# Attention value products: one piece instead of two for some key tiles

## The chip, the cores and the metric

The kernel runs on 1 core of one Trainium2 chip. The metric is the device time of one execution in microseconds (us). The engines are named as in the profile: PE (TensorE, matrix products), PEld (its weight loads), DVE (VectorE), ACT (ScalarE), POOL (GpSimd) and SP (SyncE, which issues transfers).

## The reference, cut to what matters

Four layers work on one sequence of 2048 rows of 256 numbers, each added to its input: attention (16 heads, 4 key and value heads, rotary positions, biases), a gated MLP with dequantised 4-bit weights, attention with 16 key and value heads, and the same MLP again. The change is in the attention, which for each head is

```python
scores = jnp.einsum('bhqd,bhkd->bhqk', q, k) / jnp.sqrt(hd)
scores = jnp.where(causal[None, None], scores, -inf)
attn = jax.nn.softmax(scores, axis=-1)
out = jnp.einsum('bhqk,bhkd->bhqd', attn, v)
```

Nothing in the arithmetic of the reference changes here; only how the last line is cut into instructions does.

## The kernel before, in words

**Units.** Queries are taken in four blocks `b` of 512 rows (`TB`), heads in four groups `g` of four. A pair (b, g) is a unit; each attention layer runs its 16 units in order. Keys come in tiles of 128 rows: unit (b, g) has 4(b + 1) of them, of which the last four are diagonal. A diagonal tile masks the causal triangle and has 512, 384, 256 and 128 queries left (`q0` = 0, 128, 256, 384). I call these four k0 to k3. All other tiles are full: 512 queries.

**Two sweeps.** A softmax needs the largest score of each row. `max_steps` (line 776) computes scores with queries on the partitions (L787), masks diagonal pieces (L762), and DVE takes maxima (L799). A maximum is as wide as its keys: 512 for keys of earlier blocks, 128 to 512 on the diagonal. `gather` (L811 to L822) makes the row maxima, and `turn` transposes them on PE (L835), from where ACT copies them to `mT` (L841). `value_steps` (line 848) then computes the scores again with keys on the partitions. `pair(kt, p)` handles key tile `kt` and heads 2p and 2p + 1 of the group: PE puts the negated maxima into PSUM (L884) and adds the scores (L889) and, on the diagonal, the masks (L762); ACT takes the exponential into a tile `e` (L901). One pair is two heads of 512 queries. The maxima of a unit are made beside the value sweep of the unit before it.

**Value products.** `values(half)` (line 853) multiplies the exponentials of key tile `kt - 1` with its values (L869), after `pair(kt, half)`. Four products, one for each head, write four groups of 32 rows of one accumulator `ps_av`. In the profile each of these four is two matmuls, so one call is 8 records. Before the change a tile with 384 or 512 queries is cut: `values(0)` does queries up to 256, `values(1)` the rest. A tile with 256 or 128 queries is done whole in `values(0)`. The last unit of a layer, (3, 3), which has no maxima of a next unit beside it, does all its tiles whole in `values(1)`.

**Buffers.** Score tiles of both sweeps, `ps_s`, share three buffers in PSUM, used in turn: a fourth tile waits until the exponential (ACT) or the maximum (DVE) of an earlier one has been read. `e` has four buffers, two key tiles' worth.

**Order.** It is written by hand. `run` (line 974) makes for each unit a list of main steps, two for a key tile (p = 0, 1), and a list of side steps: maxima of the next unit, preparation of the next block, the output projection. `weave` runs the scores of a main step, then its share of side steps, then `values`. No side steps fall on the last three main steps of a unit (`rest=3`): k2's second pair and both of k3. The masks of a diagonal tile are put off (`owed`) and issued at the next `settle`, which every `pair` and `values` call and some maxima begin with. The last tile's products and the copy of `ps_av` (`end`) come after the first pair of the next unit; in the last unit they follow directly, and the MLP (L1086) comes next on PE.

Of the kernel before, what the change touches and what calls it, by code (L numbers as in the profile page):

```python
# [27 lines left out]
NG = NH // 4  # L28
MLP = 2048
NFC = MLP // P  # L30
TB = 512
NB = S // TB
# [48 lines left out]
def tile_hybrid_layers(  # L81
# [40 lines left out]
    def ps_s():  # L122
        return psum.tile([P, 2, 512], F32, tag="s", name="ps_s", bufs=3)

    def ps_av():
        return psum.tile([P, 512], F32, tag="av", name="ps_av")

    def ps_m():
        return psum.tile([P, 512], F32, tag="m", name="ps_m")
# [22 lines left out]
    once = first_w.enter_context(tc.tile_pool(name="once", bufs=1))  # L152
# [258 lines left out]
    class Attention:  # L411
# [11 lines left out]
        def __init__(self, first, wqkv):  # L423
            self.first, self.wqkv = first, wqkv
            self.kvh = NKV if first else NH
            self.npair = NKV if first else NH // 2
            self.krows = self.kvh * HD
            self.kT, self.vv, self.qT, self.mT, self.att = {}, {}, {}, {}, {}
            self.q_d, self.k_d = {}, {}
            self.owed, self.after = [], []  # L430

        def place(self, pool, b):

            kvh = self.kvh
            self.kT[b] = pool.tile([P, self.npair, TB], F32R, tag=f"kT{b}", name=f"kT{b}")
            v_b = pool.tile([P, NT, kvh * VW + V_PAD], F32, tag=f"v{b}", name=f"v{b}")
            nc.gpsimd.memset(v_b[:, :, kvh * VW :], 0.0)
            ones = v_b[:, :, : kvh * VW].rearrange("p t (h c) -> p t h c", c=VW)
            nc.gpsimd.memset(ones[:, :, :, HD : HD + 1], 1.0)
            self.vv[b] = v_b  # L440
# [335 lines left out]
        def max_steps(self, b, g):  # L776

            held = {}

            def scores(i, c, p):  # L780
                if not held:
                    held["mx"] = self.wk.tile([P, NT, 4, NB], F32, tag="mx", name="mx")
                w = TB if c < b else (i + 1) * P
                self.settle("max")
                pt = ps_s()
                for r in range(2):
                    nc.tensor.matmul(  # L787
                        pt[:, r, :w],
                        lhsT=self.qT[b, g][64 * r : 64 * r + 64, p, i * P : (i + 1) * P],
                        rhs=self.key_rows(c, g, p, r, slice(0, w)),  # L790
                        start=True, stop=(c < b),
                    )

                def masked():
                    self.add_mask(pt, 0, w - P)
                    reduced()

                def reduced():
                    nc.vector.tensor_reduce(  # L799
                        held["mx"][:, i, 2 * p : 2 * p + 2, c], pt[:, :, :w], AX.X, ALU.max  # L800
                    )

                if c == b:
                    self.owed.append(("max", masked))
                else:
                    reduced()

            def gather():
                self.settle()
                nm = self.wk.tile([P, NT, 4], F32, tag="nm", name="nm")  # L810
                nc.vector.tensor_reduce(  # L811
                    nm, held["mx"][:, :, :, : b + 1], AX.X, ALU.max, negate=True
                )

                to = m_pad[:, :, :, :6].rearrange("q t r (p s) -> q t p r s", s=3)
                rest = nm.rearrange("q t (p r) -> q t p r", r=2)

                nc.vector.tensor_tensor(to[:, :, :, :, 0], rest, rest, ALU.max)
                less = self.wk.tile([P, NT, 2, 2], F32, tag="rest", name="rest")
                nc.vector.tensor_tensor(less, rest, to[:, :, :, :, 0], ALU.subtract)  # L820
                nc.vector.tensor_tensor(to[:, :, :, :, 1], less, less, ALU.max)
                nc.vector.tensor_tensor(  # L822
                    to[:, :, :, :, 2], less, to[:, :, :, :, 1], ALU.subtract
                )

            def turn():
                pt = ps_m()


                for _ in range(4 if (b, g) <= (1, 0) else 0):  # L830
                    nc.tensor.matmul(
                        pt, lhsT=sel[:, 0, :], rhs=nothing, start=True, stop=True
                    )
                for i in range(NT):
                    nc.tensor.matmul(  # L835
                        pt[:, i * P : (i + 1) * P],
                        lhsT=m_pad[:, i].rearrange("p r c -> p (r c)"), rhs=ident_b,
                        start=True, stop=True,
                    )
                self.mT[b, g] = self.wk.tile([P, TB], BF16, tag="mT", name="mT")  # L840
                nc.scalar.copy(self.mT[b, g], pt)  # L841


            tiles = [(i, c) for c in range(b + 1) for i in range(NT)]
            steps = [lambda i=i, c=c, p=p: scores(i, c, p) for i, c in tiles for p in range(2)]
            return steps + [gather], turn

        def value_steps(self, b, g):

            nk = NT * (b + 1)  # L850
            held = {"pending": []}

            def values(half):


                self.settle()
                kt, q0, es_ = held["pending"][0]
                whole = (b, g) == (NB - 1, NG - 1)
                few = whole or TB - q0 <= TB // 2
                if half == 1:  # L860
                    held["pending"].pop(0)
                if few and half != whole:
                    return
                if kt == 0 and half == whole:
                    held["av"] = ps_av()
                own = slice(q0, TB) if few else slice(*((q0, TB // 2), (TB // 2, TB))[half])
                for j in range(4):
                    h = g if self.first else 4 * g + j
                    nc.tensor.matmul(  # L869
                        held["av"][32 * j : 32 * j + 32, own],  # L870
                        lhsT=self.vv[kt // NT][:, kt % NT, h * VW : h * VW + 32],
                        rhs=es_[j // 2][:, j % 2, own],
                        start=(kt == 0 and half == whole), stop=(kt == nk - 1),
                    )

            def pair(kt, p):
                q0 = max(0, kt - NT * b) * P
                diagonal = kt >= NT * b
                keys = slice((kt % NT) * P, (kt % NT + 1) * P)
                self.settle()  # L880
                pt = ps_s()

                for r in range(2):
                    nc.tensor.matmul(  # L884
                        pt[:, r, q0:], lhsT=sel[64 * r : 64 * r + 64, p, :],
                        rhs=self.mT[b, g][64 * r : 64 * r + 64, q0:], start=True, stop=False,
                    )
                for r in range(2):
                    nc.tensor.matmul(  # L889
                        pt[:, r, q0:], lhsT=self.key_rows(kt // NT, g, p, r, keys),  # L890
                        rhs=self.qT[b, g][64 * r : 64 * r + 64, p, q0:],
                        start=False, stop=not diagonal,
                    )
                e = self.wk.tile([P, 2, TB], F32, tag="e", name="e", bufs=4)

                def masked():
                    self.add_mask(pt, 1, q0)
                    exponentials()

                def exponentials():  # L900
                    nc.scalar.activation(e[:, :, q0:], pt[:, :, q0:], AF.Exp, scale=QK_SCALE)  # L901

                if diagonal:
                    self.owed.append(("exp", masked))
                else:
                    exponentials()
                if p == 0:
                    held["es"] = [e]
                else:
                    held["pending"].append((kt, q0, held["es"] + [e]))  # L910

            def end():
                values(0)
                values(1)
                o = pre.tile([P, TB], F32, tag="o", name="o")
                nc.scalar.copy(o, held["av"])
                held["o"] = o
# [19 lines left out]
            for kt in range(nk):  # L937
                for p in range(2):
                    scored = lambda kt=kt, p=p: pair(kt, p)
                    steps.append((scored, lambda p=p: values(p)) if kt else scored)  # L940
# [296 lines left out]
```

## Time and profile before

| what | value |
|---|---|
| median of 3 runs | 1833.45 us |
| lowest and highest | 1830.45 and 1834.42 us |
| span of the profiled execution | 1830.9 us |
| time of the profiled execution beside its span | not listed apart from the span |
| PE busy | 1748.1 us, 95% |
| DVE busy | 1123.5 us, 61% |
| ACT busy | 808.1 us, 44% |
| value products (L869) | 4384 records, 350.7 us busy |
| maxima (L799) | 640, 660.3 us busy |
| exponentials (L901) | 640, 568.8 us busy |

Attention lies at about 40 to 560 us and 950 to 1490 us of the span, the MLPs after each. Busy times count an engine as busy from the start of an instruction to its modelled end. A timeline row gives the start of a group of equal instructions, how long the group lasted, engine, line, operation and tiles, the number of records, and in brackets idle time of the engine before it with what ended it. Since matmuls overlap, the cost of a group to PE is read from its start to the start of the next group.

### The profile page before, as it was taken

Reading aid. Unit: us, or ns where it says so; the run is one execution under the profiler, and the core shown is the slowest. Engines: PE = TensorE matmul, PEld = TensorE weight load, DVE = VectorE, ACT = ScalarE, POOL = GpSimd, SP = SyncE. Lnnn points to the kernel's source line nnn. Section 1 sums busy time; section 2 is a strip of 40 time slices with the busy share of each in tenths; the row PEclk is TensorE's granted clock in tenths of the full one; section 3 lists DMA queues with packets and bytes.
Section 4 is the critical chain, followed back from the end, with each engine's and each line's share of the span. In section 5 each row is a group of like instructions: output and inputs, shape, how many; then the busy total and the mean of one; then the engine's idle time right before and its main releaser. Section 6 shows DMA issues by size and latency. Waiting matters only on the chain.

```text
span 1830.9 us, 31568 instructions
## 1 busy us (share of the span) xinstructions
PE 1748.1 (95%) x13313; PEld 913.3 (50%) x13313; DVE 1123.5 (61%) x1679; ACT 808.1 (44%) x1080; POOL 239.8 (13%) x444
## 2 busy tenths in 40 slices
PE   8888899899999999999998999999999999999999
PEld 4444444444443474746464444444444445655646
DVE  5576887887884626262644767767877626354442
ACT  2435556566667313131314455655666753132221
POOL 4122202110013101012101000000000001111010
PEclk9899999999999999999999999999999999999999
DMA  5240400120002100005006132032000000000000
GB/s 139 68 93 32 94 24 30 48 50 24 19 13 76 52 1 0 1 0 125 2 1 117 24 76 53 22 60 59 13 13 2 11 37 1 12 3 9 7 6 12
DMA packets 43134, 65.40 MB, mean 36 GB/s; under 512 B 14000, under 2 KB 21040, under 8 KB 42736
## 3 DMA queue, kind: packets, MB, share of 16 engines
q1 hardware_dynamic: 34352, 47.37, 9.0%
q0 software_dynamic: 7680, 15.48, 4.9%
q8 instruction: 105, 1.72, 0.4%
q10 hardware_dynamic: 960, 0.52, 0.1%
q14 instruction: 37, 0.30, 0.1%
HBM read 43.45 MB, written 17.83 MB: 33 GB/s over the span
## 4 chain that ended last, share of the span: by engine, by line
PE 74%; DVE 15%; ACT 7%; issue 2%; DMA 1%; POOL 0%; ACTq 0%; DVEq 0%; SPq 0%; POOLq 0%
PE ps_s L1086 24%; DVE mx L799 12%; PE ps_av L869 10%; PE ps_s L884 7%; PE ps_s L787 6%; PE ps_m L1111 6%; PE ps_av L1111 6%; ACT e L901 5%; PE ps_s L889 5%; PE ps_m L504 2%; PE ps_m L963 2%; PE ps_s L762 1%; ACT mT L841 1%; PE ps_s L504 1%; PE ps_m L923 1%
## 5 line engine op out<-in xcount | busy, mean ns | idle before, releaser
L799 DVE TENSOR_REDUCE mx<-ps_s 128x2 f32<-128x1024 f32 (+3 forms) x640 | 660.3, 1061 | 216.7 <-PE ps_s L762 109.0
L901 ACT ACTIVATE e<-ps_s 128x1024 f32<-128x1024 f32 (+3 forms) x640 | 568.8, 898 | 374.1 <-PE ps_s L889 219.5
L869 PE MATMUL ps_av<-e,v 128*32 128x256 f32 (+2 forms) x4384 | 350.7, 391 | 0.0
L889 PE MATMUL ps_s<-qT,kT 64*128 64x512 f32 (+3 forms) x1280 | 333.8, 519 | 0.0
L787 PE MATMUL ps_s<-kT,qT 64*128 64x512 f32 (+3 forms) x1280 | 266.5, 418 | 34.2 <-DVE mx L799 15.3
L884 PE MATMUL ps_s<-mT,sel 64*128 64x512 bf16 (+3 forms) x1280 | 229.9, 353 | 26.1 <-ACT mT L841 11.0
L1086 PE MATMUL ps_s<-xnT,wg 128*128 128x512 f32 x512 | 240.9, 593 | 0.0
L1086 PE MATMUL ps_s<-xnT,wu 128*128 128x512 f32 x512 | 240.6, 592 | 0.0
L884 PEld LDWEIGHTS <-sel 64*128 64x128 bf16 x1280 | 75.5, 93 | 252.4 <-issue 241.8
L787 PEld LDWEIGHTS ps_s<-kT,qT 64*128 64x128 f32 x1280 | 127.6, 185 | 142.8 <-ACT e L901 67.3
L1092 ACT ACTIVATE t<-ps_s 128x512 f32<-128x512 f32 x128 | 76.3, 596 | 243.9 <-PE ps_s L1086 243.7
L1095 ACT ACTIVATE t<-t 128x512 f32<-128x512 f32 x128 | 80.6, 629 | 199.0 <-DVE t L1094 199.0
L1094 DVE TENSOR_TENSOR t<-ps_s,t 128x512 f32<-128x512 f32 x128 | 88.2, 689 | 123.3 <-POOL t L1093 121.1
L1086 PEld LDWEIGHTS ps_s<-xnT,wu 128*128 128x128 f32 x512 | 97.3, 190 | 122.5 <-issue 122.5
L1093 POOL TENSOR_SCALAR t<-t 128x512 f32<-128x512 f32 x128 | 79.0, 618 | 534.4 <-ACT t L1092 530.8
L1086 PEld LDWEIGHTS ps_s<-xnT,wg 128*128 128x128 f32 x512 | 95.1, 190 | 104.2 <-issue 102.5
L1096 DVE SCALAR_TENSOR_TENSOR t<-t,ps_s 128x512 f32<-128x512 f32 x128 | 88.0, 687 | 89.0 <-ACT t L1095 89.0
L869 PEld LDWEIGHTS ps_av<-e,v 128*32 128x32 f32 x4384 | 87.3, 108 | 93.2 <-issue 78.9
L889 PEld LDWEIGHTS ps_s<-qT,kT 64*128 64x128 f32 x1280 | 128.4, 195 | 0.0
L1111 PE MATMUL ps_m<-wd,inter 128*128 128x256 f32 x512 | 114.5, 380 | 0.0
L1111 PE MATMUL ps_av<-wd,inter 128*128 128x256 f32 x512 | 114.5, 380 | 0.0
L1111 PEld LDWEIGHTS ps_av<-wd,inter 128*128 128x128 f32 x512 | 96.7, 190 | 17.1 <-issue 4.5
(147 smaller groups left out, 1192.8 us busy)
## 6 DMA issues: line engine op xcount, KB each, us to landing
qT<-h SPq DMA_DIRECT2D x248, 64.0 KB, 2.2
kT<-h POOLq DMA_DIRECT2D x88, 128.0 KB, 5.8
h<-high SPq DMA_DIRECT2D x24, 256.0 KB, 2.1
h<-low SPq DMA_DIRECT2D x24, 256.0 KB, 3.1
wd<-wd_kept SPq DMA_DIRECT2D x2, 2048.0 KB, 8.2
wd_kept<-dq_d SPq DMA_DIRECT2D x4, 512.0 KB, 2.7
out<-x SPq DMA_DIRECT2D x16, 128.0 KB, 1.7
x<-x SPq DMA_DIRECT2D x3, 512.0 KB, 7.5
```

Source lines behind the costliest of these rows:

```text
L787: nc.tensor.matmul(pt[:, r, :w], lhsT=self.qT[b, g][64 * r : 64 * r + 64, p, i * P : (i + 1) * P], rhs=self.key_rows(c, g, p, r, slice(0, w)),
L799: nc.vector.tensor_reduce(held["mx"][:, i, 2 * p : 2 * p + 2, c], pt[:, :, :w], AX.X, ALU.max)
L869: nc.tensor.matmul(held["av"][32 * j : 32 * j + 32, own], lhsT=self.vv[kt // NT][:, kt % NT, h * VW : h * VW + 32], rhs=es_[j // 2][:, j % ...
L884: nc.tensor.matmul(pt[:, r, q0:], lhsT=sel[64 * r : 64 * r + 64, p, :], rhs=self.mT[b, g][64 * r : 64 * r + 64, q0:], start=True, stop=False,)
L889: nc.tensor.matmul(pt[:, r, q0:], lhsT=self.key_rows(kt // NT, g, p, r, keys), rhs=self.qT[b, g][64 * r : 64 * r + 64, p, q0:], start=Fals ...
L901: nc.scalar.activation(e[:, :, q0:], pt[:, :, q0:], AF.Exp, scale=QK_SCALE)
L1086: nc.tensor.matmul(pt[:, k, :], lhsT=w[:, c, fc * P : (fc + 1) * P], rhs=self.xnT[b][:, c, :], start=(c == 0), stop=(c == 1),)
L1093: nc.gpsimd.tensor_scalar(t, t, GELU_A, 1.0, ALU.mult, ALU.add)
L1094: nc.vector.tensor_tensor(t, gate, t, ALU.mult)
L1095: nc.scalar.activation(t, t, AF.Tanh, scale=GELU_C)
L1096: nc.vector.scalar_tensor_tensor(t, t, 1.0, gate, ALU.add, ALU.mult)
L1111: nc.tensor.matmul(po[:, :D], lhsT=inter[:, fc, i * P : (i + 1) * P], rhs=wd[:, fc, :], start=(fc == 0), stop=(fc == NFC - 1),)
```

## The change

A flag `wide` is set while a step issues a maximum over more than 256 keys and cleared by each `pair`. At `values(0)` it is decided how the tile is done: with fewer than 512 queries, whole in `values(0)`; with 512 queries and no wide maximum since the pair before it, whole in `values(1)`; else in two halves as before. The special case of the last unit is gone.

```diff
             def values(half):
                 self.settle()
                 kt, q0, es_ = held["pending"][0]
-                whole = (b, g) == (NB - 1, NG - 1)
-                few = whole or TB - q0 <= TB // 2
+                if half == 0:
+                    held["late"] = q0 == 0 and not self.wide
+                    held["once"] = q0 > 0 or held["late"]
                 if half == 1:
                     held["pending"].pop(0)
-                if few and half != whole:
+                if held["once"] and half != held["late"]:
                     return
-                if kt == 0 and half == whole:
+                opening = kt == 0 and half == held["late"]
+                if opening:
                     held["av"] = ps_av()
-                own = slice(q0, TB) if few else slice(*((q0, TB // 2), (TB // 2, TB))[half])
+                own = slice(q0, TB)
+                if not held["once"]:
+                    own = slice(*((0, TB // 2), (TB // 2, TB))[half])
```

In the order of the built program this joins 62 tiles: k1 (384 queries) of every unit but the last of each layer, 30 in all, now whole in `values(0)`; and 32 tiles of 512 queries outside the last units, now whole in `values(1)`. In the two last units the full tiles and k0 stay as they were, while k1 and k2, already whole, move from `values(1)` to `values(0)`, that is, one pair earlier; k3 comes in `end` as before. All other engines have the same instructions in the same order, and each score tile reuses the buffer of the same predecessor, except at one place.

More of the change, by code (lines that the diff above doesn't have):

```diff
@@ L430, in __init__ @@
             self.owed, self.after = [], []
+            self.wide = False
         def place(self, pool, b):
@@ L785, in scores @@
                 pt = ps_s()
+                self.wide = self.wide or w > TB // 2
                 for r in range(2):
@@ L872, in values @@
                         rhs=es_[j // 2][:, j % 2, own],
-                        start=(kt == 0 and half == whole), stop=(kt == nk - 1),
+                        start=opening, stop=(kt == nk - 1),
                     )
@@ L880, in pair @@
                 self.settle()
+                self.wide = False
                 pt = ps_s()
```

## Prediction

> **What bounds the kernel now.** I began with the page's busy line and its chain of work that ended last.
>
> ```profile
> PE 1748.1 (95%) x13313; PEld 913.3 (50%) x13313; DVE 1123.5 (61%) x1679; ACT 808.1 (44%) x1080; POOL 239.8 (13%) x444
> ...
> PE 74%; DVE 15%; ACT 7%; issue 2%; DMA 1%; POOL 0%; ACTq 0%; DVEq 0%; SPq 0%; POOLq 0%
> ```
>
> PE is the bound, but not alone: in the attention the chain hops over DVE maxima (12% of the span on L799) and ACT exponentials (5% on L901). The question at each joined tile is therefore whether PE was short of time there, or was filling a wait with half a tile.
>
> The price of a group comes from the PE timeline, start to next start. The last unit has whole tiles already:
>
> ```profile
> 1459.99 1.07 PE L869 MATMUL ps_av<-e,v 128*32 128x512 f32 x8
> 1460.99 0.39 PE L884 MATMUL ps_s<-mT,sel 64*128 64x512 bf16 x2
> 1461.03 0.58 PE L889 MATMUL ps_s<-qT,kT 64*128 64x512 f32 x2
> 1461.45 0.39 PE L884 MATMUL ps_s<-mT,sel 64*128 64x512 bf16 x2
> 1461.49 0.58 PE L889 MATMUL ps_s<-qT,kT 64*128 64x512 f32 x2
> 1462.00 1.07 PE L869 MATMUL ps_av<-e,v 128*32 128x512 f32 x8
> ```
>
> 512 queries cost 1.00 us (1459.99 to 1460.99). The same way, 384 cost 0.79 (1485.77 to 1486.56), 256 cost 0.57 and 128 cost 0.35. Going from scores to products costs 0.09 more than going on to the next scores: 1461.49 to 1462.00 against 1461.03 to 1461.45; after masks it is 0.16 against 0.07.
>
> **The change part by part.** *On PE alone.* A joined full tile saves 2 x 0.57 - 1.00 = 0.14, a joined k1 saves 0.35 + 0.57 - 0.79 = 0.13, and each saves one passage of 0.09: about 0.23 us. 62 tiles give 14.3 us, if PE never waits.
>
> A page speaks for more: the Trainium skill, "TensorE: Matmul & The Clock Gate", Back-to-back issue gap, gives a sustained 81 ns a matmul at 128 columns and 131 ns at 512. Interpolated to 98 ns at 256, an estimate, 16 x 98 - 8 x 131 ns is 0.52 us a tile and 32 us for 62. The rows above have 71 and 125 ns a record and decide.
>
> *The tail of a unit (30 k1 tiles).* This is (0,3,2), layer, block and group counted from 0, from k2's first pair:
>
> ```profile
> 553.47 0.28 PE L884 MATMUL ps_s<-mT,sel 64*128 64x256 bf16 x2
> ...
> 553.88 0.43 PE L869 MATMUL ps_av<-e,v 128*32 128x128 f32 x8
> 554.23 0.28 PE L884 MATMUL ps_s<-mT,sel 64*128 64x256 bf16 x2
> ...
> 554.64 0.64 PE L869 MATMUL ps_av<-e,v 128*32 128x256 f32 x8
> 555.21 0.23 PE L884 MATMUL ps_s<-mT,sel 64*128 64x128 bf16 x2
> ...
> 555.56 0.64 PE L869 MATMUL ps_av<-e,v 128*32 128x256 f32 x8
> 556.13 0.40 PE L835 MATMUL ps_m<-ident_b,m_pad 128*128 128x128 bf16 x4
> ```
>
> ```profile
> 554.81 0.60 ACT L901 ACTIVATE e<-ps_s 128x512 f32<-128x512 f32 x1 [0.17 <-PE ps_s L762]
> ```
>
> k2's products at 555.56 need the exponential of k2's second pair. It begins 0.33 after that pair's masks (554.48 to 554.81), lasts 0.60, and the half of k1 at 554.64 covers it. After the change: 384 queries at 553.88, k2's second pair at 554.67, its masks at 554.92, its exponential 555.25 to 555.85. Nothing is left between but k3's first pair: at 554.99, masks at 555.18, k2's products at 555.34. Two of their four heads need the second exponential; PE gets there at 555.62, waits until 555.90 (0.05 after the end, as PE follows ACT at 556.57 + 0.59 to 557.20), and is through at 556.19, against 556.13. So the 0.23 becomes a wait, and 0.06 is lost. Side steps can't cover it, there are none here. Of the 30 tails, 12 show PE waiting afterwards for m_pad from DVE (0.14 to 0.94 us); there it costs nothing. The other 18 cost 18 x 0.06 = 1.1 us.
>
> *The two last units.* k2's products lose the cover of k3's second pair, k3's that of k2's. Walked from 1485.07 with the same steps: k1's products 1485.47, k2's second pair 1486.26, its exponential 1486.82 to 1487.42, second half of k2's products at 1487.47, k3's second pair 1487.76, its exponential 1488.27 to 1488.65, last products until 1488.88. Before, the MLP's first matmul starts at 1488.13. That is 0.75 a layer, 1.5 us; the MLP is PE's, so nothing hides it.
>
> *The 32 full tiles.* With the first half gone, the second pair comes 0.57 + 0.09 = 0.66 earlier, if its score buffer is free. This is (1,3,1), where two narrow maxima stand behind the first pair:
>
> ```profile
> 1394.65 0.39 PE L884 MATMUL ps_s<-mT,sel 64*128 64x512 bf16 x2
> ...
> 1395.60 0.64 PE L869 MATMUL ps_av<-e,v 128*32 128x256 f32 x8
> 1396.44 0.39 PE L884 MATMUL ps_s<-mT,sel 64*128 64x512 bf16 x2 [0.20 <-ACT e L901]
> ...
> 1397.19 0.64 PE L869 MATMUL ps_av<-e,v 128*32 128x256 f32 x8
> ```
>
> ```profile
> 1395.37 1.02 ACT L901 ACTIVATE e<-ps_s 128x1024 f32<-128x1024 f32 x1 [0.49 <-PE ps_s L889]
> ```
>
> First pair and two maxima hold all three buffers; the second pair waits for the first's exponential, 1396.39, with or without a half tile at 1395.60. That half was free. Afterwards the whole tile stands at 1397.19 and costs 1.00 instead of 0.57: 0.43 lost. Five tiles are so: the late ones of (1,3,0), (1,3,1), (1,3,2), (0,2,2), (1,2,2): 2.15 us. Three more ((0,2,3), (1,2,3), (1,1,0)) lose it too, but 0.16 of it meets a wait that stands behind (404.12 + 0.46 to 404.73): 3 x 0.27 = 0.81.
>
> Where one maximum or none follows the first pair, the second pair does come 0.66 earlier, and the next maximum then waits for the first's exponential. (0,3,1), tile at 497.80: the second pair starts at 497.70 instead of 498.37, the maximum at 498.72 (exponential 497.65 to 498.67) instead of 498.83; the products move from 499.39 to 499.28 and end at 500.28; before, the next pair started at 500.17. 0.11 lost. Walked alike: (0,3,2) 0.13, (0,3,0) 0.26, (0,1,3) and (1,1,3) 0.21 each, (0,2,0) and (1,2,0), two tiles each, 0.10 for both, (1,2,1), two tiles, 0.27, (1,1,1)'s first 0.34. Together 1.73 for 12 tiles.
>
> Two tiles have long side work of PE in a step ((0,2,1) and (1,1,1)'s second) and keep the gain: -0.46. In the two at 479.58 and 526.75, DVE then has maxima queued up, PE's 0.31 is hidden: 0. (0,1,0), (0,1,1) and the six k0 tiles of block 0 stand among long preparation; each lies between -0.23 (free gain) and +0.43 (class above), I take 0, since 10 of their 16 halves lie off the chain. Full tiles: 2.15 + 0.81 + 1.73 - 0.46 = 4.2 us.
>
> Again the skill, "Perfetto Trace Analysis", Matmuls: groups should rotate through PSUM banks so that evacuation overlaps the next matmuls, and larger matmuls are more efficient. The first half is what the split did at 1395.60, the second what the change does; by the rows the first is worth 0.57 there, the second 0.14.
>
> *Sum.* 1.1 + 1.5 + 4.2 = 6.8 us on the span of 1830.9, 1837.7. The page has no other time of that execution; the median is 2.55 above its span and I keep that distance: **1840.2 us**, +0.37%. DMAs, DVE, ACT and POOL keep their instructions and order; maxima that come 0.1 to 0.5 earlier wait for nothing else.
>
> **Rivals.** *Faster: PE is the bound and takes the saving.* For it: 95% busy; 45 of the 62 tiles have a half on the chain. 45 x 0.23 = 10.4, so 1823. It decides if the exponentials that I make late are found done; against it, they need to be 0.28 (tails) to 0.6 us (full tiles) earlier, and ACT, with 44% busy, is not late by its own queue but follows PE's masks by a steady 0.33. *Same: tails gain, full tiles lose.* If the wait at 555.62 isn't there, 18 tails give -0.23 each, -4.1, against 4.2 of the full tiles, with the last units about 0: 1833.5. Point: 0.28 us of ACT. *Slower still: the clock.* TensorE's granted clock is 0.51 between 44 and 58 us and 1.00 before; the joined tiles take PE work out of just such thin stretches of block 0. One more such stretch of 14 us costs up to 7 us: 1847; one less, as much in gain. *That it doesn't do what it says* is out: the built order has the 62.
>
> **How the numbers follow.** Forecast 0.58, faster 0.12, same 0.22, clock 0.08. A measurement tells 0.2% or 3.7 us from no change: 1829.8 to 1837.1 is "same". Slower is 0.58 + 0.08 = 0.66, same 0.22, faster 0.12. The forecast's own range: tails 0 to 30 x 0.06 = 1.8, the eight open tiles -1.8 to +3.4, the rest within 2 us: 1836 to 1846. The range takes in the same case and leaves the faster one out: 1830 to 1846.
>
> **What will show it.** Records of the value products (L869, L875 after) fall by 62 x 8 = 496 to 3888. In the tail, products of 256 should split with about 0.3 us between their second and third head; at (1,3,1) the gap before the second pair should be some 0.85 us, ended by ACT; the MLP should start 0.75 later behind each last unit. I am wrong if PE's idle time by "ACT e" does not grow by some 10 us, or if the clock has other stretches below 0.6.

## The result and the profile after

The changed kernel takes 1848.07 us (median of 4 runs, 1847.57 to 1848.66). Four runs of the kernel before have a median of 1832.32 us (1830.45 to 1834.42). The ratio is 1.0088, with a 95% interval of 1.0073 to 1.0102: slower by 15.75 us, where 6.8 had been forecast.

The profiled span grew by 14.9 us, from 1830.9 to 1845.8. The page of the kernel after:

```profile
PE 1751.4 (95%) x12801; PEld 904.3 (49%) x12817; DVE 1124.6 (61%) x1679; ACT 804.9 (44%) x1080; POOL 239.8 (13%) x444
...
PE 76%; DVE 13%; ACT 8%; issue 2%; DMA 1%; POOL 0%; ACTq 0%; SPq 0%; DVEq 0%; POOLq 0%
...
L875 PE MATMUL ps_av<-e,v 128*32 128x256 f32 (+3 forms) x3888 | 355.4, 419 | 0.8 <-ACT e L908 0.8
```

PE does 496 products fewer (its line has 512 records fewer, but its weight loads fell by 496: 16 records are missing from the trace) and is busy 3.3 us *longer*; its idle time (span less busy) grew by 11.6 us, from 82.8 to 94.4. Together that is the 14.9. So there are two questions: who makes PE wait, and why do fewer products take longer? The waits of PE answer the first. The columns are waiting operation, what ended the wait, total us, times, longest. The kernel before:

```profile
PE ps_s L787 <- DVE mx L799: 15.3, 34, 1.3
PE ps_s L787 <- ACT e L901: 15.0, 36, 1.3
...
PE ps_s L884 <- DVE mx L799: 4.7, 14, 0.5
PE ps_m L835 <- DVE m_pad L822: 4.5, 10, 0.9
PE ps_s L884 <- ACT e L901: 4.2, 15, 0.6
```

The kernel after, the same view:

```profile
PE ps_s L789 <- ACT e L908: 19.1, 46, 1.3
PE ps_s L789 <- DVE mx L801: 16.8, 36, 1.3
...
PE ps_s L891 <- ACT e L908: 8.1, 16, 1.2
PE ps_s L891 <- DVE mx L801: 7.4, 20, 0.8
...
PE ps_m L837 <- DVE m_pad L824: 1.5, 4, 0.6
...
PE ps_av L875 <- ACT e L908: 0.8, 4, 0.2
```

Waits for exponentials grew by 8.8 us (19.2 to 28.0), those for maxima by 4.2, and those for `m_pad` fell by 3.0. Nearly all wait at *score* matmuls (L789, L891), which wait for a score buffer. Products themselves wait for only 0.8.

Where in the span is it? I took the times of each unit's `turn` and of each MLP's first matmul in both traces, and the growth of their difference:

| stretch | predicted | measured |
|---|---|---|
| layer 0, start and block 0 | 0 | +4.55 |
| layer 0, blocks 1 to 3 | 5.3 for both layers | +3.72 |
| layer 0, last unit | 0.75 | +1.23 |
| layer 1, block 0 | 0 | +0.34 |
| layer 1, blocks 1 to 3 | (above) | +3.89 |
| layer 1, last unit | 0.75 | +1.21 |
| sum | 6.8 | +14.94 |

Every stretch lost at least what was predicted. The extra comes from block 0 of layer 0 (4.55), from blocks 1 to 3 (2.3) and from the last units (0.9).

**The tail.** This is (0,3,2) on the PE timeline of the kernel after, from k2's first pair to `turn`, and its exponentials on ACT:

```profile
561.43 0.28 PE L891 MATMUL ps_s<-mT,sel 64*128 64x256 bf16 x2
...
561.83 0.85 PE L875 MATMUL ps_av<-e,v 128*32 128x384 f32 x8
562.62 0.28 PE L891 MATMUL ps_s<-mT,sel 64*128 64x256 bf16 x2
...
562.93 0.22 PE L891 MATMUL ps_s<-mT,sel 64*128 64x128 bf16 x2
...
563.27 1.20 PE L875 MATMUL ps_av<-e,v 128*32 128x256 f32 x8
564.41 0.40 PE L837 MATMUL ps_m<-ident_b,m_pad 128*128 128x128 bf16 x4
```

```profile
563.20 0.87 ACT L908 ACTIVATE e<-ps_s 128x512 f32<-128x512 f32 x2 [0.60 <-PE ps_s L763]
```

k2's products stand for 1.20 us, where the same 8 records took 0.64 before, and no wait is named. The single records tell why. Before, the four heads' first passes start at 555.561, 555.568, 555.575 and 555.581: side by side, 7 ns apart. After, two start at 563.273 and 563.280, their second passes at 563.513 and 563.520, and only at 563.847 and 563.854 come the other two heads, whose exponential had not been read. Each pair of heads takes the 0.57 us that all four took. The tail is 2.98 us long instead of 2.66.

**The last unit** of layer 1 loses in the same way, at k2 and again at k3, on the PE timeline after:

```profile
1500.64 1.20 PE L875 MATMUL ps_av<-e,v 128*32 128x256 f32 x8
...
1502.12 0.41 PE L875 MATMUL ps_av<-e,v 128*32 128x128 f32 x4
1502.73 0.41 PE L875 MATMUL ps_av<-e,v 128*32 128x128 f32 x4 [0.19 <-ACT e L908]
1503.07 1.13 PE L1093 MATMUL ps_s<-xnT,wg 128*128 128x512 f32 x2
```

**A full tile** of (1,3,1), the one that the prediction showed:

```profile
1407.13 0.39 PE L891 MATMUL ps_s<-mT,sel 64*128 64x512 bf16 x2
...
1408.92 0.39 PE L891 MATMUL ps_s<-mT,sel 64*128 64x512 bf16 x2 [0.77 <-ACT e L908]
...
1409.67 1.07 PE L875 MATMUL ps_av<-e,v 128*32 128x512 f32 x8
```

The half tile that had stood in the gap is gone, the gap stays until the exponential ends, and the whole tile comes behind it: 1.79 from the first to the second pair, as before (1394.65 to 1396.44), and 1.00 of products afterwards instead of 0.57.

### The profile page after: what moved, and what is told of

The parts are those of the page before. It is cut to its first block, busy times and chain, and to the rows that moved or that the text cites. A ratio compares the mean times of both kernels' runs of the same rounds, so it can differ in the third digit from the quotient of the medians.

```text
span 1845.8 us, 30560 instructions
## 1 busy us (share of the span) xinstructions
PE 1751.4 (95%) x12801; PEld 904.3 (49%) x12817; DVE 1124.6 (61%) x1679; ACT 804.9 (44%) x1080; POOL 239.8 (13%) x444
## 4 chain that ended last, share of the span: by engine, by line
PE 76%; DVE 13%; ACT 8%; issue 2%; DMA 1%; POOL 0%; ACTq 0%; SPq 0%; DVEq 0%; POOLq 0%
PE ps_s L1093 23%; PE ps_av L875 12%; DVE mx L801 10%; PE ps_s L891 7%; PE ps_s L789 6%; PE ps_m L1118 6%; PE ps_av L1118 6%; ACT e L908 5%; PE ps_s L896 5%; PE ps_m L505 2%; PE ps_s L763 2%; PE ps_m L970 2%; ACT mT L843 1%; PE ps_s L505 1%; PE ps_m L930 1%
## 5 line engine op out<-in xcount | busy, mean ns | idle before, releaser
L875 PE MATMUL ps_av<-e,v 128*32 128x256 f32 (+3 forms) x3888 | 355.4, 419 | 0.8 <-ACT e L908 0.8
L789 PE MATMUL ps_s<-kT,qT 64*128 64x512 f32 (+3 forms) x1280 | 266.3, 417 | 39.5 <-ACT e L908 19.1
L891 PE MATMUL ps_s<-mT,sel 64*128 64x512 bf16 (+3 forms) x1280 | 229.8, 353 | 32.0 <-ACT mT L843 11.0
L891 PEld LDWEIGHTS <-sel 64*128 64x128 bf16 x1280 | 75.8, 93 | 263.5 <-issue 254.2
L789 PEld LDWEIGHTS ps_s<-kT,qT 64*128 64x128 f32 x1280 | 127.7, 185 | 148.0 <-ACT e L908 70.4
L875 PEld LDWEIGHTS ps_av<-e,v 128*32 128x32 f32 x3888 | 81.2, 108 | 102.6 <-issue 78.0
L1118 PEld LDWEIGHTS ps_av<-wd,inter 128*128 128x128 f32 x512 | 96.7, 190 | 17.1 <-issue 4.5
```

What stands on the lines that cost most here:

```text
L789: nc.tensor.matmul(pt[:, r, :w], lhsT=self.qT[b, g][64 * r : 64 * r + 64, p, i * P : (i + 1) * P], rhs=self.key_rows(c, g, p, r, slice(0, w)),
L875: nc.tensor.matmul(held["av"][32 * j : 32 * j + 32, own], lhsT=self.vv[kt // NT][:, kt % NT, h * VW : h * VW + 32], rhs=es_[j // 2][:, j % ...
L891: nc.tensor.matmul(pt[:, r, q0:], lhsT=sel[64 * r : 64 * r + 64, p, :], rhs=self.mT[b, g][64 * r : 64 * r + 64, q0:], start=True, stop=False,)
L1118: nc.tensor.matmul(po[:, :D], lhsT=inter[:, fc, i * P : (i + 1) * P], rhs=wd[:, fc, :], start=(fc == 0), stop=(fc == NFC - 1),)
```

## The experiments

The variants change the decision at `values(0)`; variants 5, 10 and 11 change something else as well or instead. The rule of the kernel before, written in the terms of the changed code, is

```python
last = (b, g) == (NB - 1, NG - 1)
held["late"] = last
held["once"] = held["late"] or TB - q0 <= TB // 2
```

and the edits below say what differs from it. The kernel before was run along; its medians over the three groups of runs were 1833.04, 1833.23 and 1832.95 us. Theory A: two heads cost PE what four cost, so a late exponential in a tail costs a second group. Theory B: a pair of heads costs half a group, as I had predicted. C: the surplus is the clock ("half clock" below is a granted clock of 0.5). D, formed after the first four runs: a transfer in block 0 of layer 0 is delayed.

**1. Only k1, blocks 1 to 3.**

```diff
-held["once"] = held["late"] or TB - q0 <= TB // 2
+held["once"] = last or TB - q0 <= TB // 2 or (b > 0 and q0 > 0)
```

> Only k1 of the units in blocks 1 to 3 (24 tiles, the last units left out) is joined, in values(0). Theory A, that the wait for the exponential cuts k2's products into two groups of two heads, each as long as a group of four (0.57 us): 15 tails bound by PE lose 0.32 each, 4.8 us, and the tails that wait for m_pad nearly nothing: +4.5 to +5.5. Theory B, the prediction's, that two heads cost half of four: 15 x 0.06, +0.5 to +1.5. Rival that joining itself pays: -3 or less.

Measured: 1839.67 us, ratio 1.0043 (1.0028 to 1.0058). The edit joins 22 tiles, not 24: the records fell by 22 x 8. Of 8.06 us more span, 2.6 lie in block 0 of layer 0, where this kernel has the code of before (more on this at variant 3); the other 5.5 are in the 22 units with an edit. Of the 15 tails that run straight through, 14 lose 0.31 or 0.32 and one 0.43; those that wait for `m_pad` lose 0 to 0.1. A tail of (0,3,2):

```profile
558.24 0.28 PE L892 MATMUL ps_s<-mT,sel 64*128 64x256 bf16 x2
...
560.09 1.20 PE L876 MATMUL ps_av<-e,v 128*32 128x256 f32 x8
561.22 0.40 PE L837 MATMUL ps_m<-ident_b,m_pad 128*128 128x128 bf16 x4
```

The 1.20 and the 2.98 (558.24 to 561.22) are there with k1 alone. Theory A holds, B doesn't.

**2. Only full tiles, blocks 1 to 3** (26 tiles late).

```diff
-held["late"] = last
+held["late"] = last or (b > 0 and q0 == 0 and not self.wide)
```

> Only the 26 full tiles of blocks 1 to 3 are joined, in values(1). By what is left of the changed kernel's unit times once 0.32 is taken off for each tail bound by PE: +2 to +3.5. By the prediction's walks: +4.2. Rival, that PE takes the saving: -3 or less.

Measured: 1838.02 us, 1.0029 (1.0018 to 1.0041). The span grew by 2.84, by 3.6 in the stretches edited (layer 0's block 0 was 0.7 shorter, layer 1's 0.1). Units (1,3,0) to (1,3,2) lose 0.30 to 0.34 each, not 0.43; (1,1,1) gains 0.6 and (1,2,1) 0.3, while (0,2,1), which was to gain 0.23, loses 0.8. The predicted 4.2 is about right.

**3. Only block 0.**

```diff
-held["late"] = last
-held["once"] = held["late"] or TB - q0 <= TB // 2
+held["late"] = last or (b == 0 and q0 == 0 and not self.wide)
+held["once"] = held["late"] or TB - q0 <= TB // 2 or (b == 0 and q0 > 0)
```

> Only block 0 of both layers has the change (6 k0 and 6 k1 tiles). Theory C, the clock: stretches of half clock longer or more numerous than in the kernel before, all in the first 110 us, and +4 to +5.5. Rival, that the waits alone explain block 0 (six tails at 0.32 at most and the k0 tiles at their walks): the stretches of half clock as before, +0.5 to +2.5, shared by both layers.

Measured: 1837.87 us, 1.0031 (1.0018 to 1.0044); the span grew by 5.0, of which 4.4 lie in layer 0's block 0 and 0.3 in layer 1's. (The edit joins 6 k0 and 8 k1 tiles, not 6 and 6.) Of block 0, 20.5 us lie at half clock, 17.1 before. And 2.70 of the 4.4 come at one place, between the turns of (0,0,2) and (0,0,3). There, on the DVE and PE timelines of the kernel before:

```profile
94.04 0.68 DVE L535 TENSOR_TENSOR r<-r,turns 128x512 f32<-128x512 f32 x1
...
95.77 0.47 PE L787 MATMUL ps_s<-kT,qT 64*128 64x512 f32 x2
```

and of this variant:

```profile
97.89 0.69 DVE L536 TENSOR_TENSOR r<-r,turns 128x512 f32<-128x512 f32 x1 [2.08 <-DMA r<-r]
...
99.50 0.51 PE L789 MATMUL ps_s<-kT,qT 64*128 64x512 f32 x2 [1.88 <-DVE mx L801]
```

DVE waits 2.08 us for a transfer `r<-r` of the rotary step, the maxima queue up behind it, and PE waits 1.88 for a maximum's buffer. In the kernel before, the same matmuls (at 95.77) start without a wait. Counted from the turn of (0,0,2), they now start 2.1 us later. The DMA view of the stretch around that transfer, kernel before, 92 to 95.5 us (queues with packets, MB and share; then issues with KB and us to landing):

```profile
q1 hardware_dynamic: 320, 0.52, 54.2%
...
r<-r SPq DMA_DIRECT2D x1, 128.0 KB, 2.0
```

and this variant, 94 to 98.2 us:

```profile
q1 hardware_dynamic: 320, 0.52, 44.7%
q8 instruction: 1, 0.02, 1.4%
...
r<-r SPq DMA_DIRECT2D x1, 128.0 KB, 4.2
```

The same 320 packets, and one packet more: a load of instructions on queue q8, which had come at 87.1 us before and now comes at 95.6. In the ten traces whose block 0 has the code of before, it comes at 86.3 to 87.8. In the kernel after it comes at 95.2, `r<-r` takes 3.6, DVE waits 1.48, and the same stretch between two turns loses 2.42. That is theory D: the joined products have fewer instructions, the next load is due later, and it falls beside this transfer.

The loss of this stretch is not all D's, though. Behind the wait, from 100.3 to 103.7 us, PE is at half clock; the kernel before has no half clock between these turns. And variant 1, with the code of before here and the transfer in time, loses 2.05 in the same stretch, with 6.8 us at half clock in it:

```profile
94.58 0.68 DVE L536 TENSOR_TENSOR r<-r,turns 128x512 f32<-128x512 f32 x1
...
98.92 1.08 PE L876 MATMUL ps_av<-e,v 128*32 128x256 f32 x8
```

(1.08 us for a group that lasts 0.64 at full clock.) Variants 4, 6, 8, 9 and 10 lose 2.01 to 2.06 there in the same way. So of variant 3's 2.70, the 2.1 that are in place when PE's wait ends go with the transfer; the rest comes while the clock is halved.

**4. Only the last units.**

```diff
-held["late"] = last
-held["once"] = held["late"] or TB - q0 <= TB // 2
+held["late"] = last and q0 == 0
+held["once"] = last or TB - q0 <= TB // 2
```

> Only the two last units have the change (k1 and k2 one pair earlier). Theory A: k2's and k3's products are each cut in two, 1.2 a layer, +2.2 to +2.7. The prediction's walk: +1.5. All four runs of this call together should come to the changed kernel's +15 if the parts add up.

Measured: 1836.11 us, 1.0021 (1.0011 to 1.003). The last units lose 1.23 and 1.21, to the hundredth what the kernel after loses; the rest of the profile's 4.2 lies where nothing is edited, 2.0 of it in the stretch just named. It had been expected that the four parts add up to 15. They don't: their medians are 6.6, 5.0, 4.8 and 3.1 above the kernel before, 19.5 in all. One reason lies in blocks 1 to 3, where variants 1 and 2 together lose 9.1 and the kernel after 7.6: (0,2,1) loses 0.66 in one and 0.82 in the other, and nothing with both edits.

**5. Block 0 as in 3, with PE kept busy:** 8 small products of 64 columns ahead of one second pair behind a joined tile, into a score tile that is then overwritten.

```diff
+if b == 0 and p == 1 and (kt == 2 or kt == 1 and held["late"]):
+    for _ in range(8):
+        nc.tensor.matmul(
+            pt[:, 0, q0 : q0 + 64], lhsT=sel[:, 0, :], rhs=nothing[:, :64],
+            start=True, stop=True,
+        )
```

> The run of block 0 alone, plus eight small products of 64 columns before the score products of the second pair behind each joined tile (into the score tile, which is then overwritten): PE's instruction count is as in the kernel before. Theory D, that 128-record-wise loads of PE instructions moved from 87 to 95 us and delay the rotary transfer r<-r, for which DVE waits 2.1 us: the load comes back to about 87 us, the wait is gone, block 0 of the first layer costs 2 us less than in the run of block 0 alone in the trace. Rival, that the clock alone explains it: the wait for r<-r stays, or the time stays at +4 to +5 without it.

Measured: 1833.93 us, 1.0006 (0.9997 to 1.0016). The load on q8 is back at 86.6 us, `r<-r` lands in 2.0, and DVE doesn't wait:

```profile
93.32 0.67 DVE L536 TENSOR_TENSOR r<-r,turns 128x512 f32<-128x512 f32 x1
```

More work on PE, and most of the loss of variant 3 is gone. It fits D; but the added products also fill PE, and this trace has less half clock (13.7 us in block 0, none in the stretch that lost 2.70), so C isn't excluded by it.

**6 and 7. Which exponential should be early?** In 6, k1 whole early and k2 whole late; in 7, k1 whole late. Blocks 1 to 3 both.

```diff
-held["late"] = last
-held["once"] = held["late"] or TB - q0 <= TB // 2
+held["late"] = last or (b > 0 and q0 == 2 * P)    # 6; in 7: q0 == P
+held["once"] = last or TB - q0 <= TB // 2 or (b > 0 and q0 > 0)
```

> The run with k1 joined in blocks 1 to 3, plus k2 (256 queries) moved to values(1), behind k3's second pair. Theory A, that the loss of the tail is the cut of k2's products by the late exponential: the cut is gone, and k2's products cover the wait for mT; each tail bound by PE turns from +0.32 to about -0.5: -4 to -8 in all. Rival, that whole k1 products cost PE more by themselves: it stays slower than before, +3 or more.

> k1 joined in blocks 1 to 3, but in values(1), where the half stood that covered k2's exponential; k2 stays in values(0). Theory A: 0.23 a tail bound by PE is kept, 15 of them, -3 to -4. Theory B of half a group gives the same; the rival that joining costs by itself, +3 or more.

Measured: 6 takes 1832.1 us, 0.999 (0.9981 to 1.0); 7 takes 1830.54, 0.9986 (0.9977 to 0.9996). Both expectations were too high. In 6 eight of the nine units of layer 1 whose tails run straight through gain 0.28 to 0.64. Layer 0 is 1.0 longer there: 1.2 of it comes in (0,1,3), where this trace has 3.4 us at half clock that the kernel before has not, and up to 0.2 each in units whose tail waits for `m_pad`. In 7 a tail that runs straight through gains 0.11 to 0.31, as here in (0,3,2):

```profile
553.15 0.28 PE L892 MATMUL ps_s<-mT,sel 64*128 64x256 bf16 x2
...
553.96 0.85 PE L876 MATMUL ps_av<-e,v 128*32 128x384 f32 x8
...
555.10 0.64 PE L876 MATMUL ps_av<-e,v 128*32 128x256 f32 x8
555.67 0.40 PE L837 MATMUL ps_m<-ident_b,m_pad 128*128 128x128 bf16 x4
```

k1's 384 queries, put behind k2's second pair, cover that pair's exponential; k2's products come in one group again (0.64), and the tail is 2.52 instead of 2.66. So the same joining gains or loses by its place alone.

**8. Full tiles joined early,** whole in `values(0)` instead of `values(1)`.

```diff
-held["once"] = held["late"] or TB - q0 <= TB // 2
+held["once"] = last or TB - q0 <= TB // 2 or (b > 0 and q0 == 0 and not self.wide)
```

> The 26 full tiles of blocks 1 to 3 joined in values(0) instead of values(1). If the half in values(0) was filler of a wait for the score buffer, the whole tile fills it too and the second step is shorter: about 0.2 to 0.5 less each where the wait was, -2 to -6. If joining is what costs, as late: +2 to +3.

Measured: 1843.13 us, 1.0053 (1.0037 to 1.0068), span +10.1: my expectation was wrong by its sign. The wait moves to the second step. (1,3,1) on PE:

```profile
1405.24 1.07 PE L876 MATMUL ps_av<-e,v 128*32 128x512 f32 x8
1406.24 0.39 PE L892 MATMUL ps_s<-mT,sel 64*128 64x512 bf16 x2
...
1408.04 0.44 PE L789 MATMUL ps_s<-kT,qT 64*128 64x384 f32 x2 [0.54 <-ACT e L909]
```

The whole tile is longer than the wait it fills, the second pair comes 1.95 behind the first (1404.29 to 1406.24) instead of 1.79, and behind the second pair there is no half tile left to do while its exponential runs: PE waits 0.54. In both places a half covers an exponential.

**9. Each layer its better order:** k1 late in layer 0, k1 early and k2 late in layer 1, blocks 1 to 3.

```diff
-held["late"] = last
-held["once"] = held["late"] or TB - q0 <= TB // 2
+held["late"] = last or (b > 0 and q0 == (P if self.first else 2 * P))
+held["once"] = last or TB - q0 <= TB // 2 or (b > 0 and q0 > 0)
```

> Against the kernel before: k1 joined in blocks 1 to 3 of both layers, late in values(1) in the first layer, and in values(0) with k2 moved to values(1) in the second. By the unit times of the two runs that it is put together from, -1.0 in the first layer and -3.2 in the second: -4, faster by 0.2%. Rival, that what those traces show is the scatter of block 0: within 1 us.

Measured: 1829.56 us, 0.9981 (0.9972 to 0.999), span -3.1. Faster than before, a little less than expected.

**10. Theory A by itself.** In the last units only, where PE never waits at a full tile, the 26 tiles of 512 queries are done as heads 0 and 1 in `values(0)` and heads 2 and 3 in `values(1)`. Number of products and columns are those of before.

```diff
+pairs = last and q0 == 0
...
-for j in range(4):
+for j in (2 * half, 2 * half + 1) if pairs else range(4):
```

> Against the kernel before, with the same products and columns: in the two last units the 26 tiles of 512 queries do heads 0 and 1 in values(0) and heads 2 and 3 in values(1), each 512 columns wide. Theory A, two heads cost as much as four, since the four run side by side: 1.00 and one passage of 0.09 more for each tile, 26 x 1.09, +25 to +29. Theory B, two heads cost half: 26 x 0.09, +1 to +4.

Measured: 1861.62 us, 1.0157 (1.0138 to 1.0175). The span grew by 29.3, of which 13.77 and 13.71 in the two units, 1.06 a tile. PE timeline:

```profile
1489.91 1.05 PE L873 MATMUL ps_av<-e,v 128*32 128x512 f32 x4
1490.89 0.39 PE L889 MATMUL ps_s<-mT,sel 64*128 64x512 bf16 x2
...
1491.44 1.05 PE L873 MATMUL ps_av<-e,v 128*32 128x512 f32 x4
1492.43 0.39 PE L889 MATMUL ps_s<-mT,sel 64*128 64x512 bf16 x2
```

Two heads of 512 queries take 0.98 and 0.99 us, four took 1.00 before. Theory A is shown, with no wait in play.

**11. Theory D without work in block 0.** Variant 3, but the warm-up products at the start (22 of 512 columns) are cut into 54 of 208: about the same columns, 64 more PE instructions, so that later loads are due earlier.

```diff
-fill(22)
+for _ in range(54):
+    nc.tensor.matmul(
+        idle[:, :208], lhsT=zeros[:, :P], rhs=zeros[:, :208], start=True, stop=True
+    )
```

> The run of block 0 alone, and the 22 warm-up products of 512 columns at the start cut into 54 of 208 columns (the same columns): 64 instructions more ahead of block 0, none put into it. Theory D: the load of instructions falls near 87 us again, r<-r lands in 2 us, DVE does not wait for it, and 2 us of the cost of block 0 go. Rival, that PE's emptier block 0 is the cause by way of the clock: the cost stays at +4 to +5.

Measured: 1834.52 us, 1.0004 (0.9995 to 1.0013), clear of variant 3's interval. The load comes at 91.1 us, `r<-r` lands in 2.0, DVE waits for nothing, and the stretch that lost 2.70 in variant 3 loses 0.00:

```profile
98.03 0.68 DVE L536 TENSOR_TENSOR r<-r,turns 128x512 f32<-128x512 f32 x1
```

This variant's one profile, 1836.86 us, is its slowest run. It is 4.0 us longer in block 0, with 27 us at half clock, all ahead of that stretch. Its other runs go down to 1830.64.

Like variant 5's, this trace has no half clock in the stretch itself, so it doesn't part D from C alone. The mean clock that every run recorded does, by an estimate. The 64 runs of the kernel before that were taken with the variants lie near a line: 1834.3 to 1834.8 us at a clock of 0.993, 1832.3 to 1833.1 at 0.995, 1830.1 to 1831.5 at 0.997, about 0.9 us for each 0.001. Compared at the same clock, variant 3 is 3.5 us slower than the kernel before, variant 5 2.0 and variant 11 1.4 (the kernel after 13.4). So of variant 3's 4.8 us some 1.5 to 2.1 go with the late transfer, in line with the 2.1 of its trace, and about 1.3 with the clock. The 1.4 to 2.0 that variants 5 and 11 still lose have no cause shown.

**12. The best of all:** variant 9, and full tiles late in three units that had been shorter in the kernel after.

```diff
-held["late"] = last or (b > 0 and q0 == (P if self.first else 2 * P))
+held["late"] = last or (b > 0 and q0 == (P if self.first else 2 * P)) or (
+    q0 == 0 and not self.wide
+    and (self.first, b, g) in ((True, 2, 1), (False, 2, 1), (False, 1, 1)))
-held["once"] = last or TB - q0 <= TB // 2 or (b > 0 and q0 > 0)
+held["once"] = held["late"] or TB - q0 <= TB // 2 or (b > 0 and q0 > 0)
```

> The run with k1 and k2 moved, and in the three units with long side work of PE, (0,2,1), (1,1,1) and (1,2,1), the full tiles joined late as in the changed kernel, where their units were 0.3, 0.5 and 0.3 shorter: 1 us less than that run, -5 against the kernel before. If those gains belonged to the waits that are now gone: no better than that run.

Measured: 1827.78 us, 0.997 (0.9959 to 0.998), span -4.1. It beats both kernels; what the late tiles of the three units add to variant 9 is not clear of the runs' scatter (the two intervals overlap). In the traces (1,1,1) is 0.6 and (1,2,1) 0.3 shorter than in variant 9, but (0,2,1) is 0.2 longer.

## Why the prediction was right or wrong

**Right: the direction, and that the tails, the full tiles and the last units lose by late exponentials.** The records fell to 3888. Cover was lost as said, and waits for "ACT e" grew by 8.8 us, with 10 named as the test. The gap at (1,3,1) was to be 0.85 and ended by ACT; it is 0.77 and ended by ACT. The full tiles were put at 4.2; alone the 26 outside block 0 cost 3.6. That sum came out partly by luck, since its parts are off both ways: three of them lose 0.3 where I had 0.43, (1,2,1), given as losing 0.27, gains 0.3, and (0,2,1), given as gaining 0.23, loses 0.8.

**Wrong: the step "Two of their four heads need the second exponential; PE gets there at 555.62, waits until 555.90 ..., and is through at 556.19".** I divided a group's 0.57 by two. Two heads take all of it, so PE is not at the second pair of heads at 555.62 but at 555.34 + 0.57 = 555.91; there is no wait left, and it is through at 555.91 + 0.57 = 556.48. That is 0.35 behind the 556.13 of before, instead of 0.06; variant 1 measured 0.31 or 0.32 in 14 of 15 tails. This also refutes the named sign, "split with about 0.3 us between their second and third head": it was 0.57. The last units fail by the same step: 0.29 more at k2 (half of 0.57) and 0.17 more at k3 (half of 0.35) turn my 0.75 into 1.21; measured 1.23 and 1.21. It accounts for the 0.9 of the last units, and for most of the surplus in blocks 1 to 3: variant 1's 5.5 us and variant 2's 3.6 are 9.1 apart, 7.6 together, where I had 5.3.

The rows could have told it, since 8 records of 0.27 us or more within 0.64 can't run one after the other. The Trainium skill has it as a rule: "TensorE: Matmul & The Clock Gate", Part 3, Measured speedup vs the span model, gives a pack of small matmuls the time of one, plus about 4 ns for each further one. The rows here show 7 ns from start to start. By that rule, as an estimate, two products of a pack of four cost as much as all four to within 0.01 us, and the estimate of a tail would have been right.

**Wrong: "the six k0 tiles of block 0 ... I take 0" and "DMAs, DVE, ACT and POOL keep their instructions and order".** They keep their order, but not their times. In the list of DMA queues I passed over q8, the loads of instructions, on the page of the kernel before and then of the kernel after:

```profile
q8 instruction: 105, 1.72, 0.4%
```

```profile
q8 instruction: 101, 1.65, 0.4%
```

A load moved from 87.1 to 95.2 us and met the rotary transfer. Variant 3 against 5 and 11 (+0.31% against +0.06% and +0.04%) shows that most of the loss goes when the load is put elsewhere, some of it by way of the clock. That the load slows the transfer rests on all 14 traces together. They have 252 transfers `r<-r`. The 17 slowest (3.3 to 4.7 us) all have a load that starts 1.2 to 2.5 us behind their issue, and of the 223 with no load in them none took more than 3.03. Twelve others with a load in them took 1.9 to 2.9, so not every load beside a transfer slows it, and no run moves a load by itself. Nor does every slow transfer cost PE time: in variants 7, 8 and 10 one of unit (0,0,1) took 3.9 to 4.2 us, and the stretch between the turns around it is no longer than before.

**The rivals.** The one called "the clock" gave 1847, near the 1848.07, but not by what it said. There was no further stretch of 14 us: half clock in block 0 went from 17.1 to 23.9 us. A stretch below 0.6 that the kernel before has not, my own sign of being wrong, is there (100.9 to 104.3 us), but a small one. Kernels whose block 0 has the code of before show 10.2 to 27.3 us there, and pass (0,1,0) between 0.7 us earlier and 2.7 later than the kernel before. Of the 4.55 us in the kernel after, 2.4 lie in the stretch of the transfer: 1.45 are in place when PE's wait ends at 99.27, and the rest comes with 3.4 us at half clock behind it, from 100.9. The other 2.1 lie where its longer half-clock stretches are, within that scatter. Whether the change makes such stretches likelier stays open: all four runs of the kernel after have a mean clock of 0.992 or 0.993, as only 11 of 64 runs of the kernel before have, but variant 11, with the same thin PE work in block 0, has 0.993 to 0.998. "Faster: PE is the bound" falls with every stretch that lost. "Same" needed that the wait at 555.62 isn't there. It isn't, and yet the tail loses, by the cost of the second group.

## What to carry to other kernels

Matmuls that run side by side, as the four heads here, have one price for the group: a wait that cut the group in two doubled it, so find the operand that comes last before moving such a group, or count it twice. A piece of work that stands in a wait is free there and costs its full time elsewhere; before joining two pieces, look at what each one covers (here each half covered an exponential, and the joined tile paid where it moved earlier and where it moved later). When the number of instructions changes, look in the DMA queues for the loads of instructions, and for the transfers on the path beside which they then fall. Where the clock moves, compare runs at the same clock.

## What the runs showed of the hardware that was not expected

- Two heads of 32 output rows each cost PE what four cost: 0.57 us at 256 queries, 0.98 at 512, 0.34 at 128 (1502.73 to 1503.07).
- A load of instructions is a 16 KB packet on a queue of its own; between 60 and 120 us of the kernel before they come 10 to 19 us apart. Where one came beside the 128 KB transfer at (0,0,2), the transfer took 3.6 and 4.2 us instead of 2.0.
- The stretches at half clock come in multiples of 3.41 us (3.41, 6.83, 10.24, 13.65, 17.07), and their number differs between runs of the same instructions: in block 0 of layer 0, 10.2 to 27.3 us in all, with -0.7 to +2.7 us of span. Single profiles that differ by less than that in block 0 tell nothing.
